# Four graph layers on one core: orders and product forms in the first slices, and layer 3's three weights applied before its first product

## The chip, the cores and the metric

The kernel runs on one core of a Trainium2 chip. The metric is the device time of one execution in microseconds (us); the median of several executions is given with the lowest and the highest. In the profile PE is TensorE's matrix multiplication, PEld its weight loads, DVE the VectorE, ACT the ScalarE, POOL the GpSimd, SP the SyncE, which here only issues transfers. PSUM is the memory into which PE sums, in eight banks of 512 fp32 values for each of 128 partitions.

## The reference, cut to what matters

x is 8 x 2048 x 64 (batch, nodes, features) and adj, called A, is 2048 x 2048 with rows that sum to 1. Everything is fp32. Four layers follow each other, each with a residual and a layernorm over the 64 features:

```python
x = _layernorm(x + _L0_gnn_ref(x, adj, L0_gnn_embedding, L0_gnn_weight, L0_gnn_bias), axis=-1)
x = _layernorm(x + _L1_gnn_ref(x, 0, L1_gnn_net_params, adj), axis=-1)
x = _layernorm(x + _L2_gnn_ref(x, adj, L2_gnn_weight_self, L2_gnn_weight_neighbor, L2_gnn_bias), axis=-1)
x = _layernorm(x + _L3_gnn_ref(x, adj, adj, L3_gnn_weight, L3_gnn_bias), axis=-1)
```

Layer 0 takes x, Ax and 2AAx - x through weights that differ by node. Layer 1 is relu(A x W) twice. Layer 2 is x Wself + (A x) Wneigh + b. Layer 3 is this, with adj for both supports:

```python
x0 = inputs_and_state
x_stack = [x0]
for support in (support0, support1):
    x1 = jnp.einsum('ij,bjk->bik', support, x0)
    x_stack.append(x1)
    x_prev, x_curr = (x0, x1)
    for _ in range(2, K + 1):
        x2 = 2.0 * jnp.einsum('ij,bjk->bik', support, x_curr) - x_prev
        x_stack.append(x2)
        x_prev, x_curr = (x_curr, x2)
x_cat = jnp.concatenate(x_stack, axis=-1)
out = jnp.einsum('bnf,fo->bno', x_cat, weight) + bias
```

With the five 64 x 64 parts W0 to W4 of its weight and both supports alike, layer 3 is x (W0 - W2 - W4) + A x (W1 + W3) + A A x 2 (W2 + W4) + b. The kernel calls these three weights W3X, W3A and W3AA. All weights have their mean over the outputs taken away, so that a layernorm needs no mean, and the identity is added to the weight of x, which gives the residual.

## The kernel before

**Where things lie.** x lies in SBUF by nodes: `xy[:, slot, t, col]`, 128 nodes on the partitions, t one of 16 node tiles, col the 8 x 64 columns of batch and feature; slot 0 and 1 are two such arrays. A pair `p` is two batches (128 columns), a group `g` four node tiles (512 nodes). `part(g, p, slot)` is one 128 x 512 piece.

**Products.** Every A times X is 2048 x 2048 by 2048 x 512. `product` does it in two levels of the seven-product method (Strassen-Winograd): seven quarter products, in the order A11, S1, A12, S2, S4, S3, A22, and in each, `inner` with seven `mul`s. Each `mul` loads one 1 MB block of adj, or of a sum of adj blocks, from DRAM (`comb`, made in the first stage) on SP's queue; seven such buffers are in flight in the later layers. Thus one product is 49 `mul`s. A `mul` has two forms. The form at L277 is 4 matmuls 512 wide with x as the loaded weight; its result is by features and has to go through a weight (`project`) to come back to nodes. The form at L270 (`onto_slot`) is 16 matmuls 128 wide with adj as the loaded weight; its result is by nodes and is added to what already lies in an xy slot. A matmul of the program is two instructions in the trace.

**Order on PE.** Small jobs (transposes, projections) are Python generators in a queue, the pump. After each `mul` the pump takes `rate` steps, so jobs come between the blocks of a product. That order is PE's order in the built program. `prior` adds the jobs of `own` to the pump, one for each quarter of the output.

**First stage (0 to 212 us).** The first A X is made in four slices `ns`, each of 512 output columns, while DVE makes the sums of adj blocks (`prepare`, line L640, names `si` for inner sums and `so` for outer ones) and POOL stores them to `comb`. adj arrives in 1 MB chunks on SP's queue (L158), x on ACT's and SP's (L169, L172). Slice 0 (`plain_slice`) is half plain matmuls (L872), half `two_level` (L832, 28 matmuls 128 wide). Slices 1 to 3 (`fast_slice`) have seven quarter products: A12, A22, A11, S1, S2, S4, S3, of which A22 is by `two_level` and the others are 16 matmuls 256 wide for each of two pairs (L918). `prepare` is a generator; each `next(parts)` lets DVE's queue have the next group of sums. The results hT go back to nodes by transposes (L465), those of the last slice's first pairs after the slice.

**Layer 2 and 3.** `both_terms` (L1177) takes two pairs: it transposes each (L1152, four transposes into one PSUM bank `pt`, copied to SBUF as `xT`), multiplies the upper and the lower 64 rows by two weights of 64 columns side by side (L1190, 16 pairs of half-row matmuls into four banks), and ACT copies one result to slot 0 (L1195), DVE adds the bias to the other and writes slot 1 (L1196). Layer 3 uses `w3o` with W3A for slot 0 and W3X for slot 1. Its first product, of slot 1 in the 512-wide form, gives A x by features; `feature3` (L1213) projects that by W3AA and adds it to slot 0, which then holds x W3A + (A x) W3AA. Its second product, of slot 0 in the 128-wide form, adds A times that to slot 1. `ends` gives the last quarter a special end (layernorm and store piece by piece). PSUM has three banks for the products and five for these jobs (`p_z`).

**Weights.** `load_weights` and `sum_weights` (L594 to L629) build seven 128 x 128 weights `wd` (the 64 x 64 weight twice on the diagonal) and copy four of them into `w2o` and `w3o`; they run on DVE in slice 1.

Of the kernel before, what the change touches and what calls it, by code (L numbers as in the profile page):

```python
# [16 lines left out]
P = 128  # L17
EPS = 1e-5
GW = 512
# [85 lines left out]
def kernel(  # L105
# [58 lines left out]
    AHEAD = (2, 3, 0, 1)  # L164
    chunks[0, AHEAD[0]] = slice_chunk(0, AHEAD[0], (1, 1, 2))

    for t, n, cols in ((0, 1, slice(0, 2 * F)), (0, 1, slice(2 * F, BF)), (1, 1, slice(0, BF)), (2, 2, slice(0, BF))):
        t += AHEAD[0] * TG
        nc.scalar.dma_start(xy[:, 0, t : t + n, cols], x[:, t : t + n, cols])  # L169
# [7 lines left out]

    W1A, W1B, W2N, W2S, W3X, W3A, W3AA = range(7)
    wd = const.tile([P, 7, P], F32, tag="wd", name="wd")

    w3o = const.tile([P, 2, F], F32, tag="w3o", name="w3o")
    w2o = const.tile([P, 2, F], F32, tag="w2o", name="w2o")
    b2 = const.tile([P, F], F32, tag="b2", name="b2")
    b3 = const.tile([P, F], F32, tag="b3", name="b3")
# [400 lines left out]
    if True:  # L585
# [8 lines left out]
        def load_weights():  # L594
            nc.gpsimd.memset(wd, 0.0)
            w3 = sums.tile([P, 5, F], F32, tag="t", name="w3", bufs=5)
            for k in range(2):
                half = slice(k * F, (k + 1) * F)
                for i, src in ((W1A, w_l1[0]), (W1B, w_l1[1]), (W2N, w_neigh), (W2S, w_self)):
                    nc.sync.dma_start(wd[half, i, half], src)  # L600
                nc.scalar.dma_start(w3[half], w_l3.rearrange("(k i) o -> i k o", i=F))
            nc.sync.dma_start(b2, b_l2.to_broadcast([P, F]))
            nc.sync.dma_start(b3, b_l3.to_broadcast([P, F]))
            return w3

        def sum_weights(w3):
            pin = tc.keep_in_program_order

            for k in range(2):
                half = slice(k * F, (k + 1) * F)  # L610
                pin(nc.vector.tensor_tensor(wd[half, W3A, half], w3[half, 1], w3[half, 3], ALU.add))
                pin(nc.vector.tensor_tensor(w3[half, 2], w3[half, 2], w3[half, 4], ALU.add))
                pin(nc.vector.tensor_tensor(wd[half, W3X, half], w3[half, 0], w3[half, 2], ALU.subtract))
                pin(nc.vector.tensor_scalar(wd[half, W3AA, half], w3[half, 2], 2.0, None, ALU.mult))


            for k in range(2):
                half = slice(k * F, (k + 1) * F)
                center(wd[half, W2N:, half], half, pin=pin)
            for w in (W2S, W3X):  # L620
                pin(nc.vector.tensor_tensor(wd[:, w, :], wd[:, w, :], ident, ALU.add))
            for k in range(2):
                half = slice(k * F, (k + 1) * F)
                for n, w in enumerate((W3A, W3X)):
                    pin(nc.vector.tensor_copy(w3o[half, n], wd[half, w, half]))
                for n, w in enumerate((W2N, W2S)):
                    pin(nc.vector.tensor_copy(w2o[half, n], wd[half, w, half]))
            center(b2.unsqueeze(1), pin=pin)
            center(b3.unsqueeze(1), pin=pin)  # L629
# [4 lines left out]
        def prepare(ns, ch, outers):  # L634
# [50 lines left out]
            yield  # L685
            inner(A12, *raw(0, 1))
            if ns == 0:

                sums_of_blocks()
                outers[A11] = inner(A11, *raw(0, 0))  # L690
                outers[A21] = inner(None, *raw(1, 0))
# [7 lines left out]
            put(S1, s1)  # L699
            yield  # L700
            put(S2, s2)
            if ns:
                inner(A11, *raw(0, 0))
            yield
            if ns:
                outers[S3] = s3 = outer(rq(0, 0), rq(1, 0), ALU.subtract)
                yield
            put(S3, s3)
            if ns == 0:
                yield  # L710
            put(S4, s4)
            yield

        with tc.tile_pool(name="p_n", bufs=4, space=PSUM) as p_n, tc.tile_pool(
# [92 lines left out]
            ]  # L807
            t1 = [[by_tiles(xy[:, 1, c:NT:TG, ts(n, 2 * F)]) for n in range(4)] for c in range(2)]
            b4 = [T[3][:, 2 * j : 2 * j + 2, :, ts(p, 2 * F)] for j in range(2) for p in range(2)]
# [86 lines left out]
            def fast_slice(ns, ch, held, rest):  # L896
# [16 lines left out]

                def mul(ps, a, b, start=True, steps=2):

                    for p in range(2):
# [6 lines left out]
                        if p < steps:  # L923
                            pump.step()
                    return ps
# [31 lines left out]
                next(parts)  # L957
                pa = mul(bank(), raw(0, 0), x_of(0, 0))
                p1 = sums.tile([P, GW], F32, tag="p1", name="p1")
                nc.scalar.copy(p1, pa)  # L960
                nc.vector.tensor_tensor(q3, q3, p1, ALU.add)
# [13 lines left out]
                nc.vector.tensor_tensor(u2, pc, u2, ALU.add)  # L975
                nc.vector.tensor_tensor(p1, pc, p1, ALU.add)
                next(parts)
                pe = mul(bank(), summed(S4), x_of(1, 1))
                done(1, pe, u2)
                if ns == TG - 1:  # L980
                    join_bias(1, 0)
                mul(pb_, summed(S3), t_of(3), start=False)

                done(2, pb_, q3)
                done(3, pb_, p1)
                return [hT[p] for p in range(NP)]

            last_pairs = []
            for ns in range(TG):
                ch = [chunks.pop((ns, j)) for j in range(NG)]  # L990
                if ns == 0:
# [15 lines left out]
                    hT = next(first4)  # L1007
                    next(parts)
                    w3 = load_weights()
                    load_chunks(1, *AHEAD)  # L1010
                    pump.add(biases())
                else:
                    hT = fast_slice(ns, ch, held, parts if ns == 1 else ())
                for p in range(NP):
                    keep_t1(ns, p, hT[p])

                held = []
                for p in range(NP):
                    if ns == TG - 2:
                        held.append((ns, p, hT[p]))  # L1020
                    elif ns == TG - 1 and p >= NP // 2:
                        last_pairs.append(hT[p])
                    else:
                        pump.add(back(ns, p, hT[p]))
            join_bias(1, 1)
# [111 lines left out]

    late = p_z = None

    def to_late():  # L1140
# [5 lines left out]
        p_mm2 = ctx.enter_context(tc.tile_pool(name="p_mm2", bufs=1, space=PSUM))  # L1146
        p_z = ctx.enter_context(tc.tile_pool(name="p_z", bufs=5, space=PSUM))

    def pair_transposed(g, p, slot):
        pt = p_z.tile([P, GW], F32, tag="z", name="pt2")  # L1150
        for k in range(TG):
            nc.tensor.transpose(pt[:, ts(k, P)], xy[:, slot, g * TG + k, ts(p, 2 * F)], ident)  # L1152
        xT = late.tile([P, GW], F32, tag="xT", name="xT", bufs=2)
        nc.scalar.copy(xT, pt)
# [48 lines left out]
    def nothing(g, p, c):  # L1203

        yield from ()


    product(1, then(feature1b, 0, mean=True, after=both_terms(0, w2o, b2)), rate=2)
    product(0, then(nothing, 1), onto_slot=1)


    def feature3(g, p, hT):
        nc.vector.tensor_tensor(part(g, p, 0), project([(hT, W3AA)]), part(g, p, 0), ALU.add)  # L1213
        yield

    product(1, feature3, own=both_terms(1, w3o, b3), rate=1.5)
    product(0, then(nothing, 1, single=[(1, 0)], store=True), rate=2, onto_slot=1, ends=True)
    pump.drain()
# [47 lines left out]
```

## Time and profile before

| what | value |
| --- | --- |
| median of 3 executions | 1666.83 us (1666.49 to 1666.88) |
| profiled execution | 1666.76 us |
| its span | 1665.0 us |
| granted clock of TensorE, mean | 0.999 |
| bytes moved by DMA | 391.56 MB |
| first stage, first A X | 0 to 212 us |
| layer 0's second product with its weights | 212 to 736 us |
| layer 1, two products | 736 to 1092 us |
| layer 2's product | 1092 to 1276 us |
| layer 3's first product | 1276 to 1482 us |
| layer 3's second product and end | 1482 to 1665 us |

A line of the timeline has start, duration, engine, source line, operation, output<-inputs by the program's names, the shape (rows and columns of the loaded weight, then output), and how many instructions in a row it stands for; square brackets give the idle time before it and what ended it. A window line has, for each engine, its busy time and instructions, then the granted clock, the DMA share and GB/s. A DMA line has the queue, the number of transfers, their size and the median time from issue to landing in us.

### The profile page before, as it was taken

How to read it: one execution, taken by the hardware profiler on the slowest of the kernel's cores; microseconds unless marked ns; L12 is line 12 of the kernel's file. 1: busy time of each engine (PE TensorE's matmuls, PEld its weight loads, DVE VectorE, ACT ScalarE, POOL GpSimd, SP SyncE). 2: the span in 40 equal slices, each digit the busy share in tenths (PEclk: the TensorE clock that was granted, in tenths of full speed). 3: DMA queues.
4: the chain of work that ended last, by engine and by line, in shares of the span. 5: the costliest groups of instructions: out<-in, count | busy, mean ns of one | idle time of the engine just before them, and what ended most of it. 6: DMA issues, size and time to landing. Idle time of an engine off the chain costs nothing.

```text
span 1665.0 us, 21271 instructions
## 1 busy us (share of the span) xinstructions
PE 1656.7 (100%) x8414; PEld 1060.6 (64%) x8414; DVE 965.9 (58%) x1737; ACT 276.0 (17%) x810; POOL 246.1 (15%) x332
## 2 busy tenths in 40 slices
PE   9999999999999999999999999999999999999998
PEld 5988844444444444444454455599998455579998
DVE  5986895656456456655434365873668344453657
ACT  0200110242142144430010011220001011100001
POOL 1221200254155056550000000000000000000000
PEclk9999999999999999999999999999999999999999
DMA  8998899504503600019877867657888866678884
GB/s 318 340 383 310 316 322 326 200 26 162 205 26 129 250 26 26 26 65 364 290 266 278 304 254 257 229 218 272 291 297 299 306 209 233 230 264 294 316 311 167
DMA packets 81074, 391.56 MB, mean 235 GB/s; under 512 B 8944, under 2 KB 25584, under 8 KB 41040
## 3 DMA queue, kind: packets, MB, share of 16 engines
q1 hardware_dynamic: 68288, 346.78, 58.2%
q0 software_dynamic: 11248, 42.08, 6.7%
q10 hardware_dynamic: 1440, 1.35, 0.3%
q8 instruction: 67, 1.10, 0.3%
q14 instruction: 31, 0.25, 0.0%
HBM read 339.85 MB, written 50.33 MB: 234 GB/s over the span
## 4 chain that ended last, share of the span: by engine, by line
PE 95%; DVE 3%; DMA 1%; issue 0%; SPq 0%; DVEq 0%
PE y L1109 20%; PE mmb L277 17%; PE mma L277 12%; PE mmc L277 12%; PE mmb L270 9%; PE ps_n L918 7%; PE mma L270 6%; PE mmc L270 6%; PE z L1161 3%; PE z L1190 2%; PE ps_i L832 1%; DVE si L640 1%; DMA xy<-in_x 1%; PE pt L1152 1%; DMA bias<-in_b_l 0%; DVE so L640 0%
## 5 line engine op out<-in xcount | busy, mean ns | idle before, releaser
L277 PE MATMUL mmb<-a,t 128*128 128x512 f32 x648 | 292.0, 593 | 0.0
L1119 DVE SCALAR_TENSOR_TENSOR xy<-y,e_sb,xy 128x128 f32<-128x128 f32 x512 | 179.6, 351 | 141.2 <-PE y L1109 125.3
L277 PEld LDWEIGHTS mmb<-a,t 128*128 128x128 f32 x648 | 121.5, 190 | 145.3 <-issue 143.5
L1128 POOL TENSOR_TENSOR s<-s 128x512 f32<-128x512 f32 (+2 forms) x192 | 157.4, 820 | 333.0 <-ACT s L1123 322.8
L1123 ACT ACTIVATE s<-y,e_sb 128x128 f32<-128x128 f32 x512 | 139.3, 383 | 231.5 <-PE y L1109 231.5
L228 DVE TENSOR_TENSOR u<-mmb,p 128x512 f32<-128x512 f32 x84 | 57.9, 689 | 176.5 <-PE mmb L277 121.1
L270 PE MATMUL mmb<-t,a 128*128 128x128 f32 x1344 | 156.9, 275 | 0.0
L270 PEld LDWEIGHTS mmb<-t,a 128*128 128x128 f32 x1344 | 153.5, 192 | 0.0
L1109 PE MATMUL y<-wn,xT 64*128 64x512 f32 x512 | 131.5, 590 | 0.0
L1109 PE MATMUL y<-wn,C 64*128 64x512 f32 x512 | 131.2, 589 | 0.0
L1109 PE MATMUL y<-wn,tT 64*128 64x512 f32 x512 | 131.2, 589 | 0.0
L277 PE MATMUL mma<-a,T 128*128 128x512 f32 x256 | 115.5, 594 | 0.0
L277 PE MATMUL mmc<-a,t 128*128 128x512 f32 x216 | 97.3, 592 | 0.0
L295 ACT COPY p<-mma 128x512 f32<-128x512 f32 x42 | 24.7, 588 | 405.8 <-PE mma L277 248.4
L1109 PEld LDWEIGHTS y<-wn,xT 64*128 64x128 f32 x512 | 49.3, 187 | 61.2 <-issue 60.7
L1109 PEld LDWEIGHTS y<-wn,tT 64*128 64x128 f32 x512 | 49.6, 187 | 60.2 <-issue 60.2
L1109 PEld LDWEIGHTS y<-wn,C 64*128 64x128 f32 x512 | 49.5, 187 | 60.3 <-issue 60.3
L277 PE MATMUL mma<-a,xy 128*128 128x512 f32 x192 | 86.6, 594 | 0.3 <-PE pt_n L465 0.3
L277 PEld LDWEIGHTS mma<-a,T 128*128 128x128 f32 x256 | 47.6, 190 | 56.8 <-issue 56.5
L228 DVE TENSOR_TENSOR C<-mmc,C 128x512 f32<-128x512 f32 x48 | 33.2, 692 | 85.9 <-PE mmc L277 75.1
L277 PEld LDWEIGHTS mmc<-a,t 128*128 128x128 f32 x216 | 40.0, 190 | 45.4 <-issue 45.2
L277 PEld LDWEIGHTS mma<-a,xy 128*128 128x128 f32 x192 | 36.0, 190 | 44.4 <-issue 43.8
(160 smaller groups left out, 2127.5 us busy)
## 6 DMA issues: line engine op xcount, KB each, us to landing
a<-comb SPq DMA_DIRECT2D x240, 1024.0 KB, 4.8
a<-in_blocks SPq DMA_DIRECT2D x54, 1024.0 KB, 4.8
comb<-si POOLq DMA_DIRECT2D x28, 1024.0 KB, 6.2
a<-in_slices SPq DMA_DIRECT2D x15, 1024.0 KB, 9.0
comb<-so POOLq DMA_DIRECT2D x15, 512.0 KB, 9.6
t1T<-hT SPq DMA_DIRECT2D x16, 256.0 KB, 4.6
xT<-in_xT SPq DMA_DIRECT2D x16, 256.0 KB, 3.0
tT<-t1T SPq DMA_DIRECT2D x16, 256.0 KB, 3.1
```

Source lines behind the costliest of these rows:

```text
L228: nc.vector.tensor_tensor(out, a, b, op)
L270: nc.tensor.matmul(to, a[:, k, m, :], xb[:, m, :], start=(start and opens and m == 0), stop=(m == TG - 1), skip_group_check=True,)
L277: nc.tensor.matmul(ps, xb[:, m, :], a[:, :, m, :], start=(start and m == 0), stop=(m == TG - 1), skip_group_check=True,)
L295: nc.scalar.copy(p1, pa)
L640: tc.keep_in_program_order(nc.vector.tensor_tensor(out, a, b, op))
L918: nc.tensor.matmul(ps[:, ts(p, GW // 2)], b(k, p), a(k // TG, k % TG), start=(start and p == k == 0), stop=(k == NT // 2 - 1), skip_group_ ...
L1109: mm = nc.tensor.matmul(y[:, b, :], terms[n][half, ts(k, P)], wn[half, n, h * DH : (h + 1) * DH, :], start=(n == 0), stop=(n == 2),)
L1119: nc.vector.scalar_tensor_tensor(acc, y[:, :, ts(d, F)], e, acc, ALU.mult, ALU.add)
L1123: nc.scalar.activation(s[:, d], y[:, :, ts(d, F)], AF.Copy, scale=e)
L1128: nc.gpsimd.tensor_tensor(s[:, :n], s[:, :n], s[:, n : 2 * n], ALU.add)
L1161: nc.tensor.matmul(z[:, k, :], aT[:, ts(k, P)], wd[:, w, :], start=(n == 0), stop=(n == len(terms) - 1),)
L1190: nc.tensor.matmul(z[n][:, k], xT[half, ts(k, P)], w[half], start=True, stop=True)
```

## The change

In the first stage: the first adj chunk comes in pieces of 1 and 3 tiles (before: 1, 1, 2), and x's tiles 1 to 3 of the first chunk in one transfer of 768 KB (before: 256 and 512 KB). In slice 0, `put`, which makes and stores the inner sums, comes in the order S1, S3, S2, S4; S2 and S4 are made while slice 1 begins. In slice 1, A11 goes through `two_level` as A22 does, so its inner sums are made earlier. In the last slice S3 comes ahead of S4, and the transposes of pairs 0 and 1 are stepped inside S4's matmuls. `wd` keeps two weights; `w2o` and `w3o` are loaded and summed where they are used, `w3o` with three weights.

In layer 3: `three_terms`, stepped from the pump after layer 2's layernorm of each pair, transposes a pair, multiplies it by the three weights W3AA, W3A, W3X side by side (192 columns) in upper and lower row halves, copies x W3AA to slot 0 and x W3A to slot 1 (ACT), adds the bias to x W3X (DVE) and stores that to DRAM (`x3`, POOL's queue, 16 x 256 KB). The first product is then A (x W3AA), in the 128-wide form, added to slot 1. Meanwhile x3 is loaded to slot 0 (POOL's queue). The second product is A times slot 1, added to slot 0. PSUM is shared out anew: while `three_terms` runs, one bank for transposes and two tiles of two banks for sums; afterwards two banks. `xT` and `rest` share three buffers.

```diff
-    chunks[0, AHEAD[0]] = slice_chunk(0, AHEAD[0], (1, 1, 2))
-    for t, n, cols in ((0, 1, slice(0, 2 * F)), (0, 1, slice(2 * F, BF)), (1, 1, slice(0, BF)), (2, 2, slice(0, BF))):
+    chunks[0, AHEAD[0]] = slice_chunk(0, AHEAD[0], (1, 3))
+    for t, n, cols in ((0, 1, slice(0, 2 * F)), (0, 1, slice(2 * F, BF)), (1, 3, slice(0, BF))):
...
             inner(A12, *raw(0, 1))
+            if ns == 1:
+                outers[A11] = inner(A11, *raw(0, 0))
...
             put(S1, s1)
             yield
+            if ns == 0:
+                put(S3, s3)
+                yield
             put(S2, s2)
-            if ns:
+            if ns > 1:
                 inner(A11, *raw(0, 0))
...
-                pa = mul(bank(), raw(0, 0), x_of(0, 0))
-                p1 = sums.tile([P, GW], F32, tag="p1", name="p1")
-                nc.scalar.copy(p1, pa)
+                p1 = new_out("p1")
+                if ns == 1:
+                    two_level(
+                        lambda i, j: lambda m: ch[j][:, m, i], outers[A11], b1[0], t1[0], by_blocks(p1)
+                    )
+                else:
+                    pa = mul(bank(), raw(0, 0), x_of(0, 0))
+                    nc.scalar.copy(p1, pa)
...
                 if ns == TG - 1:
+                    nc.vector.tensor_tensor(q3, pb_, q3, ALU.add)
+                    next(parts)
+                    ps3 = mul(bank(), summed(S3), t_of(3))
+                    done(2, ps3, q3)
+                    for p in range(2):
+                        keep_t1(ns, p, hT[p])
+                        pump.add(back(ns, p, hT[p]))
+                    done(3, ps3, u2)
                     join_bias(1, 0)
-                mul(pb_, summed(S3), t_of(3), start=False)
+                    pe = mul(bank(), summed(S4), x_of(1, 1), n=2)
+                    done(1, pe, u2)
...
+    def to_wide():
+        nonlocal p_z, p_zz
+        banks_z.close()
+        p_z = banks_z.enter_context(tc.tile_pool(name="p_z1", bufs=1, space=PSUM))
+        p_zz = banks_z.enter_context(tc.tile_pool(name="p_zz", bufs=2, space=PSUM))
...
+    def three_terms(g, p):
+        tiles = tiles_of(g)
+        xT = pair_transposed(g, p, 1)
+        yield
+        for q in range(2):
+            rest = late.tile([P, GW], F32, tag="xT", name="rest", bufs=3)
+            rest4 = rest.rearrange("p (a b n f) -> p a b n f", a=2, b=2, n=2)
+            zs = [p_zz.tile([P, 2, GW], F32, tag="zz", name="zz") for _ in range(2)]
+            zs = [z[:, :, : 6 * F].rearrange("p a (b n f) -> p a b n f", b=2, n=3) for z in zs]
+            for k in range(TG):
+                for n in range(2):
+                    half = slice(n * F, (n + 1) * F)
+                    nc.tensor.matmul(
+                        zs[n][:, k // 2, k % 2], xT[half, ts(k, P)], w3o[half], start=True, stop=True
+                    )
+            if q == 0:
+                xT = pair_transposed(g, p + 1, 1)
+            for n, z in enumerate(zs):
+                cols = ts(2 * (p + q) + n, F)
+                for slot in range(2):
+                    to = xy[:, slot, tiles, cols].rearrange("p (a b) f -> p a b f", b=2)
+                    nc.scalar.copy(to, z[:, :, :, slot])
+                nc.vector.tensor_tensor(
+                    rest4[:, :, :, n], z[:, :, :, 2],
+                    b3.unsqueeze(1).unsqueeze(1).to_broadcast([P, 2, 2, F]), ALU.add,
+                )
+            nc.gpsimd.dma_start(x3[g, p + q], rest)
+            yield
...
-    product(0, then(nothing, 1), onto_slot=1)
-    def feature3(g, p, hT):
-        nc.vector.tensor_tensor(part(g, p, 0), project([(hT, W3AA)]), part(g, p, 0), ALU.add)
+    product(0, then(nothing, 1, after=three_terms), to_wide, rate=1.5, onto_slot=1)
+    def rest_of(g, p):
+        for q in range(2):
+            nc.gpsimd.dma_start(part(g, p + q, 0), x3[g, p + q].rearrange("p (t c) -> p t c", t=TG))
         yield
-    product(1, feature3, own=both_terms(1, w3o, b3), rate=1.5)
-    product(0, then(nothing, 1, single=[(1, 0)], store=True), rate=2, onto_slot=1, ends=True)
+    product(0, nothing, own=rest_of, onto_slot=1)
+    product(1, then(nothing, 0, single=[(1, 0)], store=True), to_ends, rate=2, onto_slot=0, ends=True)
```

## The prediction

> **What bounds the kernel now.** I read the busy times first, then the chain, then stage windows, and last the timelines of TensorE around each edited place.
>
> ```profile
> PE 1656.7 (100%) x8414; PEld 1060.6 (64%) x8414; DVE 965.9 (58%) x1737; ACT 276.0 (17%) x810; POOL 246.1 (15%) x332
> ...
> PE 95%; DVE 3%; DMA 1%; issue 0%; SPq 0%; DVEq 0%
> ```
>
> TensorE (PE) is busy 1656.7 of 1665.0 us and holds 95% of the chain. What is not PE is small: 1.06 us at the start, two short waits shown below, and the 6.7 us of layernorm and store after the last product. So a change is worth what it adds to or takes from PE's row of instructions, plus the waits it makes. DVE's 3% of the chain lies at 24 to 69 us: the sums of adj blocks in the first slices. The stage in which layer 3 now starts:
>
> ```profile
> 1276.30:1482.30 206.00, 206.00 (x835) 108.84 (x834) 94.77 (x158) 26.24 (x61) 0.00 (x0) 1.00 0.70 251
> ```
>
> The columns are PE (busy, after the window's sum), weight loads, DVE, ACT, POOL, granted clock, DMA share, GB/s. PE is full at clock 1.00, DVE is 46% busy (94.77/206), ACT 13%, POOL idle, the DMA engines 70%. Work moved to DVE, ACT or POOL here is covered by PE unless PE waits for a buffer of it. Three places on PE:
>
> ```profile
> 1276.28 3.60 PE L277 MATMUL mma<-a,xy 128*128 128x512 f32 x8
> 1324.35 3.60 PE L277 MATMUL mma<-a,xy 128*128 128x512 f32 x8
> ...
> 1360.56 1.05 PE L1161 MATMUL z<-wd,C 128*128 128x128 f32 x8
> 1361.45 1.04 PE L1152 MATMUL pt<-ident,xy 128*128 128x128 f32 x8
> 1362.33 3.60 PE L277 MATMUL mmb<-a,t 128*128 128x512 f32 x8
> 1365.86 2.06 PE L1190 MATMUL z<-w3o,xT 64*128 64x128 f32 x32
> 1367.84 3.70 PE L277 MATMUL mma<-a,T 128*128 128x512 f32 x8
> 1371.38 1.04 PE L1152 MATMUL pt<-ident,xy 128*128 128x128 f32 x8
> ...
> 1504.61 3.74 PE L270 MATMUL mmc<-xy,a 128*128 128x128 f32 x32
> 1533.20 3.74 PE L270 MATMUL mma<-xy,a 128*128 128x128 f32 x32
> ```
>
> Starts matter here, not durations, since matmuls overlap. From 1276.28 to 1324.35 are 14 loaded blocks in the 512-wide form: 48.07/14 = 3.434 us each. From 1504.61 to 1533.20 are 8 in the 128-wide form: 28.59/8 = 3.574 us. A projection z<-wd,C costs 1361.45 - 1360.56 = 0.89, four transposes 1362.33 - 1361.45 = 0.88 us. From 1362.33 to 1371.38 are two blocks and one set of layer 3's row-half products (16 pairs, each a product on the upper and one on the lower 64 rows): 9.05 - 2 x 3.434 = 2.18 us.
>
> **Layer 3: what goes.** Sixteen projections by W3AA: 16 x 0.89 = -14.2 us. Eight sets of row-half products: 8 x 2.18 = -17.4 us. The 64 transposes remain (16 x 0.88 both ways).
>
> **Layer 3: what comes.** The first product there, 49 blocks, turns from the 512-wide into the 128-wide form: 49 x (3.574 - 3.434) = +6.9 us. `three_terms` brings 16 sets of 4 pairs with 192 columns (three weights at once). The trace has no 192-wide pair. Below it: 128-wide matmuls start every 0.1117 us (at 68 us, 56 in 6.25 us), and 16 pairs at that pitch are 1.79 us, which leaves 2.18 - 1.79 = 0.39 us for going into the 64-row form and back. Above it, in the first stage:
>
> ```profile
> 97.28 13.98 PE L918 MATMUL ps_n<-so,xy 128*128 128x256 f32 x64
> 111.09 3.62 PE L918 MATMUL ps_n<-a,xy 128*128 128x256 f32 x16
> ```
>
> 64 matmuls of 256 columns in 13.81 us are 0.2158 each. A matmul of the program is two instructions here, and in the 64-row form upper and lower run side by side, so 8 matmuls are 8 steps of such a pitch. Midway for 192 columns: 0.1637. One set: 8 x 0.1637 + 0.39 = 1.70 us, 16 sets +27.2 us. Bounds: no 0.39 at each set (21.0 us), or the 256-column pitch throughout (33.9 us). I take the middle, because the edge was seen in each of the eight old sets and 192 lies halfway.
>
> The Trainium skill, TensorE: Matmul & The Clock Gate, section on LDWEIGHTS, gives a load's time by its columns alone, about 107 ns for 128 of them, whatever its rows. Two loads for each half-row pair would then be 213 ns against 164 of streaming, and my estimate from that page is another 16 x 8 x 0.049 = 6.3 us. The row speaks against it: the old pairs start every 112 ns with two loads each. Left out of the sum.
>
> So layer 3 by counts is -14.2 - 17.4 + 6.9 + 27.2 = +2.5 us: the count of matmuls falls, but the edge is paid 16 times in place of 8, and the 128-wide form costs 0.14 us a block.
>
> **Layer 3: emptying PSUM.** `three_terms` has two tiles of two banks for the sums (upper, lower), and one bank for transposes, where there were five banks in one pool. The old block empties like this:
>
> ```profile
> 1367.94 0.65 ACT L1195 COPY xy<-z 128x256 f32<-128x256 f32 x2 [0.24 <-PE z L1190]
> ...
> 1367.77 1.41 DVE L1196 TENSOR_TENSOR xy<-z,b 128x256 f32<-128x256 f32 x4
> ```
>
> Copies start 0.27 us apart, each 0.38; four adds in 1.41. A new set needs four copies and two adds: after its last product 0.30 + 3 x 0.27 + 0.38 = 1.49 us for ACT, and some 0.4 for DVE's add behind it, so about 1.95. Where a block of the product (3.57) stands between two sets, that is covered. In the built order one pair of sets in the quarter tile 01 and one in 11 has only four transposes and two matmuls between, about 1.2 us: 0.75 us of wait each. DVE may be in a 0.69 us add just then (half the time: 2 x 0.17), and twice a transpose finds the single bank not yet copied (0.3 each). Sum 1.5 + 0.3 + 0.6 = +2.4 us, bounds 0 and 6 (both sets waiting for a full DVE queue of four adds). If this cover goes elsewhere too, each of the 14 others costs up to 1.9.
>
> **Put at nothing.** DVE gets 32 adds and loses 32 adds and 16 of feature3; ACT gets 64 copies and loses 32: covered at 46% and 13% busy. POOL gets 16 stores of `rest` and 16 loads of 256 KB, 8.4 MB, beside 70 to 77% DMA share. The loads of x3 land in slot 0 ahead of additions in the next product's quarters; POOL has nothing else queued then. SP's queue of 1 MB blocks is seven deep, 7 x 3.5 = 25 us ahead, so a slower block isn't felt. Without that cover 8.4 MB at 251 GB/s would be 33 us of DMA time. Fewer DVE operations on weights (6 to 4 us, in slice 1) and the joined PSUM pools touch no PE work.
>
> **First slices.** Slice 1's A11 changes from 16 matmuls of 256 columns x 2 (32 x 0.2158 = 6.91) to `two_level` (56 x 0.1117 = 6.25): -0.7. Two waits go:
>
> ```profile
> 69.37 1.13 PE L832 MATMUL ps_i<-si,t 128*128 128x128 f32 x8 [0.31 <-DVE si L640]
> ...
> 211.71 3.67 PE L277 MATMUL mma<-a,xy 128*128 128x512 f32 x8 [0.27 <-PE pt_n L465]
> ```
>
> The first was 0.48 late against a pitch of 0.89 (start to start 1.37). S4's sums now go behind the slice, so A22's come 2.5 us sooner: -0.5. What is late next is A11: its sums are made on DVE at 75.4 in place of these first `so`:
>
> ```profile
> 75.41 2.35 DVE L640 TENSOR_TENSOR so<-a 128x1024 f32<-128x1024 f32 x2
> ```
>
> Two 0.69 us sums after it put the second at about 76.8 where PE wants it at 75.4: +1.1 to 1.5. The second wait (211.71 - 209.99 = 1.72 against 0.87) goes because pairs 0 and 1 are transposed inside the last S4: -0.8. At the start, x tiles 1 to 3 come in one 768 KB transfer:
>
> ```profile
> xy<-in_x ACTq DMA_DIRECT2D x1, 512.0 KB, 10.2
> xy<-in_x ACTq DMA_DIRECT2D x1, 256.0 KB, 8.0
> ```
>
> Tile 1 landed at 9.7 us and PE used it at 9.9, so a common transfer that lands with or after the old 512 KB one (12.3) could hold PE by 0 to 2.5 us. Such a hold gives DVE the same time, so it and A11's wait are not added: the larger counts, and I take +1.3 for both (0 to 2.5). Slices together: -0.7 - 0.5 - 0.8 + 1.3 = -0.7 us.
>
> **Sum.** +2.5 + 2.4 - 0.7 = +4.2 us. The profiled execution took 1666.76 us, span 1665.0 and 1.76 around it; the median of the runs is 1666.83, 0.07 above. 1666.8 + 4.2 = 1671.0 us. A run of this kernel can tell about 0.2% (3.3 us) from no change.
>
> **Rivals.**
> No change: PSUM is emptied in time, since DVE is more than half idle, and A11's sums perhaps aren't late. The sum is then 2.5 - 0.7 = 1.8, or 0.5 without the late A11: 1667.3 to 1668.6 us. For it: 46% DVE. Against: DVE was 98% busy up to 120 us, where A11's sums lie, and two sets stand too close to each other. Chance 0.27.
> Slower by the stores: transposed pairs and `rest` share three buffers, so the second following add waits until a store has landed. From a set's end at +2.0 us to the add that wants the buffer at +7.05 are 5 us. A 256 KB store on POOL took:
>
> ```profile
> comb<-so POOLq DMA_DIRECT2D x15, 256.0 KB, 9.8
> ```
>
> That is in the first stage at DMA share 0.91; near 4 us in the quiet one. At 9.8, two close sets cost 4.9 each and three spaced ones 1.3 each: +13, so 1684 us. It decides from about 5 us. Late stages stand at 0.70 to 0.77, between the two. Chance 0.15. The Trainium skill, DMA: Bandwidth & Descriptors, on POOL's transfers, gives about 2 us and bytes by 436 GB/s: an estimate of 2.6 us by that page, with which this case never happens.
> Faster: the 0.39 us edge isn't paid by new sets, which stand beside transposes in part, and nothing waits. 27.2 becomes 21.0, the stall 0: 4.2 - 6.2 - 2.4 = -4.4, so 1662.4 us. It decides below an edge of about 0.05 us a set. Against: the edge stood in each old block, beside a full product block on both sides. Chance 0.08.
>
> **How the numbers follow.** The forecast, slower by pitch and edges, has 0.50, and rivals 0.27, 0.15, 0.08. Slower by over 0.2%: 0.50 + 0.15 = 0.65; within: 0.27; faster: 0.08. The range runs from 1665.5, below no change, to 1680, into the stores' case; the forecast's own is 1669 to 1675.
>
> **What would show it.** Sets of `zz` 1.70 us on PE between neighbours; blocks of layer 3's first product 3.57 us apart; waits of `zz` on DVE's `rest` add below 1 us each in quarters 01 and 11 and nowhere else; one wait of about 1 us at A11 in slice 1; no gap at 210 us; DMA share up by 0.02 to 0.05 in the late stages. Wrong it is if sets cost under 1.4 us or over 2.1, if PE waits at every set, or if the first matmuls wait for x beyond 2.5 us.

## The result and the profile after

The changed kernel took 1676.82 us (median of 4 executions, 1675.69 to 1679.03) against 1666.74 us before: ratio 1.0061, 95% interval 1.0048 to 1.0074. That is 10 us slower, on the side that was forecast and inside the full range of 1665.5 to 1680 us, but above the forecast's own 1669 to 1675 us and more than twice the 4.2 us of the sum. The profiled execution took 1676.06 us, its span is 1674.3 in place of 1665.0 us: +9.3 us. So these 9.3 us can be followed line by line; the rest up to the median is differences between executions, which are taken up below.

The page's busy times and chain:

```profile
PE 1658.6 (99%) x9486; PEld 1154.0 (69%) x9486; DVE 966.9 (58%) x1729; ACT 286.0 (17%) x848; POOL 265.9 (16%) x364
...
PE 23%; DVE 0%; ACT 0%; issue 0%; DVEq 0%
```

PE's busy time rose by only 1.9 us, so 7.4 of the 9.3 us are time in which PE stood still: 15.7 us now, 8.3 before. The chain adds up to 23%, so it was followed back over the last quarter of the span and breaks off there. It can't be used for the rest. The list of PE's waits (what waited, for what, us in total, times, longest) covers the whole span:

```profile
PE ps_n L872 <- DMA xy<-in_x: 3.3, 2, 1.8
PE zz L1253 <- DVE rest L1263: 1.8, 2, 1.7
PE ps_i L832 <- DVE si L637: 1.7, 1, 1.7
PE rise L724 <- DVE zero L721: 1.1, 1, 1.1
PE mma L278 <- PE ps_n L918: 0.9, 1, 0.9
PE ps_i L832 <- ACT part L836: 0.4, 1, 0.4
```

Four waits are new: for x at the very start, for A11's sums (`si`) and a bank copy in slice 1, and in layer 3 for the addition `rest`. The start of the same piece of work in both timelines of PE shows where the time came in:

| start of, us | before | after | later by |
| --- | --- | --- | --- |
| bias products, slice 1 | 62.51 | 65.16 | 2.65 |
| A11 of slice 1 | 74.80 | 76.90 | 2.10 |
| layer 1's first product | 211.71 | 215.94 | 4.23 |
| layer 2's product, one and the same place | 1086.70 | 1090.93 | 4.23 |
| last matmul | 1658.15 | 1667.68 | 9.53 |

Between 216 and 1091 us nothing changed. The first stage cost 4.2 us, for which -0.7 was forecast, and layer 3 cost 5.3 us, for which +4.9 was forecast. PE's timeline at A11 and, below, DVE's at the same time, with the issue of one store on POOL:

```profile
76.90 1.06 PE L832 MATMUL ps_i<-a,xy 128*128 128x128 f32 x8
78.31 0.49 PE L832 MATMUL ps_i<-a,xy 128*128 128x128 f32 x2 [0.35 <-ACT part L836]
80.49 1.16 PE L832 MATMUL ps_i<-si,xy 128*128 128x128 f32 x8 [1.69 <-DVE si L637]
...
85.73 3.62 PE L918 MATMUL ps_n<-so,T 128*128 128x256 f32 x16
```

```profile
75.91 0.69 DVE L637 TENSOR_TENSOR si<-a,si 128x512 f32<-128x512 f32 x1
79.02 0.69 DVE L637 TENSOR_TENSOR si<-a 128x512 f32<-128x512 f32 x1 [2.43 <-DMA comb<-si]
79.74 0.69 DVE L637 TENSOR_TENSOR si<-si,a 128x512 f32<-128x512 f32 x1
...
71.82 0.75 POOL L646 DMA_DIRECT2D comb<-si  x1 [1.78 <-DVE si L637]
```

A11 took 85.73 - 76.90 = 8.83 us, 1.9 more than the 6.91 of the old form, where 0.7 less was forecast. Without waits it would be 6.25 us, so its waits cost 2.6. The second `si` ends at 80.43 and PE goes on at 80.49. DVE itself stood still for 2.43 us ahead of A11's sums: they need one of four buffers, and that one was S2's, whose store was issued on POOL at 71.82 and landed at 78.99 us by its semaphore. So the sums were late because of a store, not because DVE had too much to do.

At the end of the first stage another wait changed. Before, then after, DVE's last additions there and PE's first weight load of layer 1's product:

```profile
210.87 0.75 DVE L934 TENSOR_TENSOR hT<-ps_n,p 128x256 f32<-128x256 f32 x2
211.68 0.30 PEld L277 LDWEIGHTS mma<-a,xy 128*128 128x128 f32 x2 [0.48 <-PE pt_n L465]
...
215.09 0.75 DVE L934 TENSOR_TENSOR hT<-ps_n,u 128x256 f32<-128x256 f32 x2 [0.17 <-PE ps_n L918]
215.91 0.30 PEld L278 LDWEIGHTS mma<-a,xy 128*128 128x128 f32 x2 [1.26 <-PE ps_n L918]
```

The profile names PE's own last work as what ended the wait, but that had ended 0.24 us earlier before and 0.86 us earlier after. In all thirteen profiles the load starts 0.07 us after the second of DVE's additions, which take the last product out of PSUM. So the product waits for DVE to empty those banks, in both orders. In the new order no transposes fill this time: from the start of PE's last matmul to that of the next are 1.27 us, 1.05 above the pitch of 0.22, where before 0.85 were lost. These pieces add up to the first stage's 4.2 us: 2.65 at the start, -0.55 for A22's wait, 1.9 at A11, 0.2 here.

In layer 3 one set of `three_terms` between blocks of the product, and the one long wait:

```profile
1276.38 0.61 PE L271 MATMUL mma<-T,a 128*128 128x128 f32 x4
1278.67 1.90 PE L1253 MATMUL zz<-w3o,xT 64*128 64x192 f32 x16 [1.68 <-DVE rest L1263]
...
1283.72 3.74 PE L271 MATMUL mmb<-t,a 128*128 128x128 f32 x32
1287.39 1.57 PE L1253 MATMUL zz<-w3o,xT 64*128 64x192 f32 x16
1288.89 3.84 PE L271 MATMUL mmc<-t,a 128*128 128x128 f32 x32
1292.56 3.74 PE L271 MATMUL mmb<-t,a 128*128 128x128 f32 x32
```

From 1283.72 to 1292.56 are two blocks and one set: 8.84 - 2 x 3.574 = 1.69 us for the set, where 1.70 was worked out. The wait stands where it was expected: after the set at 1274.38 come only four transposes and two matmuls. DVE's timeline shows what it waited for:

```profile
1275.67 0.68 DVE L229 TENSOR_TENSOR u<-mmb,p 128x512 f32<-128x512 f32 x1
1276.27 0.68 DVE L229 TENSOR_TENSOR t<-xy,t 128x512 f32<-128x512 f32 x1
1276.87 0.68 DVE L229 TENSOR_TENSOR C<-C,u 128x512 f32<-128x512 f32 x1
1277.59 0.69 DVE L229 TENSOR_TENSOR C<-xy,C 128x512 f32<-128x512 f32 x1
1278.19 0.75 DVE L1263 TENSOR_TENSOR rest<-zz,b 128x256 f32<-128x256 f32 x2
```

The set's last product had ended at 1275.95; the two `rest` additions stood behind four others in DVE's queue.

### The profile page after: what moved, and what is told of

Same layout as the page of the kernel before. It is cut to its first block, busy times and chain, and to the rows that moved or that the text cites. A ratio compares the mean times of both kernels' runs of the same rounds, so it can differ in the third digit from the quotient of the medians.

```text
span 1674.3 us, 23571 instructions
## 1 busy us (share of the span) xinstructions
PE 1658.6 (99%) x9486; PEld 1154.0 (69%) x9486; DVE 966.9 (58%) x1729; ACT 286.0 (17%) x848; POOL 265.9 (16%) x364
## 5 line engine op out<-in xcount | busy, mean ns | idle before, releaser
L271 PE MATMUL mmb<-t,a 128*128 128x128 f32 x2016 | 236.0, 275 | 0.0
L271 PEld LDWEIGHTS mmb<-t,a 128*128 128x128 f32 x2016 | 230.4, 192 | 0.2 <-issue 0.2
L278 PE MATMUL mmb<-a,t 128*128 128x512 f32 x480 | 215.8, 592 | 0.0
L278 PEld LDWEIGHTS mmb<-a,t 128*128 128x128 f32 x480 | 90.3, 190 | 109.5 <-issue 108.5
L271 PE MATMUL mma<-T,a 128*128 128x128 f32 x768 | 90.0, 275 | 0.0
L271 PEld LDWEIGHTS mma<-T,a 128*128 128x128 f32 x768 | 87.8, 192 | 0.3 <-issue 0.2
L278 PE MATMUL mma<-a,T 128*128 128x512 f32 x192 | 86.5, 593 | 0.0
L271 PE MATMUL mmc<-t,a 128*128 128x128 f32 x672 | 78.7, 275 | 0.0
L271 PEld LDWEIGHTS mmc<-t,a 128*128 128x128 f32 x672 | 76.7, 192 | 0.5 <-issue 0.5
L278 PE MATMUL mmc<-a,t 128*128 128x512 f32 x160 | 72.1, 592 | 0.0
```

Of the source, the lines that this page charges most:

```text
L271: nc.tensor.matmul(to, a[:, k, m, :], xb[:, m, :], start=(start and opens and m == 0), stop=(m == TG - 1), skip_group_check=True,)
L278: nc.tensor.matmul(ps, xb[:, m, :], a[:, :, m, :], start=(start and m == 0), stop=(m == TG - 1), skip_group_check=True,)
```

## The experiments

Eleven more kernels were run. Each time is a median beside runs of before on the same chip (1666.4 to 1666.7 us). "First product" is the start of layer 1's first product in the profile, "the rest" from there to the last matmul.

| kernel | median us (lowest to highest) | ratio to before, 95% | first product | the rest |
| --- | --- | --- | --- | --- |
| before | 1666.4 to 1666.7 | | 211.71 | 1446.44 |
| after | 1676.82 (1675.69 to 1679.03) | 1.0061 [1.0048, 1.0074] | 215.94 | 1451.74 |
| layer3_only | 1671.21 (1670.94 to 1672.73) | 1.0027 [1.0016, 1.0038] | 211.13 | 1451.75 |
| slices_only | 1672.62 (1670.76 to 1672.96) | 1.0033 [1.0020, 1.0045] | 217.48 | 1446.44 |
| old_start | 1675.23 (1674.55 to 1676.36) | 1.0053 [1.0039, 1.0066] | 214.53 | 1451.75 |
| a11_first | 1673.17 (1672.86 to 1674.98) | 1.0040 [1.0027, 1.0053] | 214.82 | 1451.75 |
| a12_last | 1670.73 (1669.81 to 1672.24) | 1.0026 [1.0016, 1.0036] | 209.47 | 1453.32 |
| adj_merged | 1673.10 (1671.44 to 1673.22) | 1.0034 [1.0021, 1.0048] | 211.47 | 1453.34 |
| x_merged | 1672.65 (1670.88 to 1673.82) | 1.0037 [1.0023, 1.0051] | 210.57 | 1453.33 |
| rest_on_act | 1670.38 (1670.21 to 1671.06) | 1.0024 [1.0015, 1.0032] | 210.87 | 1451.08 |
| all_mended | 1669.91 (1669.19 to 1671.40) | 1.0019 [1.0011, 1.0028] | 209.71 | 1451.08 |
| slices_mended | 1665.45 (1665.22 to 1666.29) | 0.9995 [0.9986, 1.0004] | 210.07 | 1446.44 |
| slices_mended_old_end | 1665.87 (1665.09 to 1666.16) | 0.9996 [0.9987, 1.0005] | 210.62 | 1446.44 |

**The two halves apart.** layer3_only is before with the change's weights and layer 3; slices_only is before with the change's first stage.

> The first stage of before with layer 3 of the change. Theory (the two parts are separate; in the profile of after the part from layer 2's product to the end took 5.3 us more on PE and the tail 0.2 less): 1666.7 + 5.1 = 1671.8 us, one PE wait of 1.7 us at a zz set behind DVE's rest. Rival (the late part's size depends on what the first stage left, such as the transfers of the sums): more than 1 us off that.

> The first stage of the change with layer 3 of before. Theory: layer 1's product starts 4.2 us later than before (2.65 at the first x tiles, 2.4 at A11's sums in slice 1, less the shorter A11 and A22's wait), and nothing of it is made up: 1666.7 + 4.2 = 1670.9 us. If the spread of the changed kernel's times (1675.7 to 1679.0) comes from the transfers at the start and at A11, this one has the spread and layer3_only has not.

layer3_only came to +4.65 us. Its rest is 1451.75 us, that of after to a hundredth, so layer 3's cost of 5.3 us does not depend on the first stage. Its first stage is 0.6 us shorter than before, because the old wait for A22's sums is gone in this profile. That is no gain of the change: an x transfer landed 0.66 us earlier, DVE, which waits for it, went on at 23.10 in place of 23.76 us, and A22's sums started 0.66 us earlier. The weight operations that DVE no longer has come later, from some 94 us on. In rest_on_act, with the same first stage, PE came 1.0 us earlier and the wait is back with 0.5 us. slices_only came to +6.06 us, 1.7 more than expected, and its profile says why. This is PE in slices_only (start, duration, instructions, wait) and then windows of it (PE, weight loads, DVE, ACT, POOL, granted clock, DMA share, GB/s):

```profile
7.43 2.84 PE L875 MATMUL ps_n<-a,xy 128*128 128x512 f32 x6 [0.24 <-DMA xy<-in_x]
12.31 12.24 PE L875 MATMUL ps_n<-a,xy 128*128 128x512 f32 x24 [2.03 <-DMA xy<-in_x]
```

```profile
12.30:13.20 0.90, 0.89 (x2) 0.46 (x3) 0.00 (x0) 0.66 (x1) 0.00 (x0) 1.00 1.01 383
13.20:14.20 1.00, 1.00 (x3) 0.44 (x2) 0.00 (x0) 0.62 (x1) 0.00 (x0) 0.52 1.04 395
14.20:15.20 1.00, 1.00 (x3) 0.48 (x2) 0.12 (x1) 0.00 (x0) 0.00 (x0) 0.50 1.01 406
15.20:16.20 1.00, 1.00 (x2) 0.41 (x2) 0.97 (x2) 0.00 (x0) 0.00 (x0) 0.50 1.11 418
16.20:17.20 1.00, 1.00 (x3) 0.32 (x2) 1.00 (x3) 0.00 (x0) 0.00 (x0) 0.77 0.89 328
```

After the wait of 2.03 us the granted clock fell to 0.50 for some 3.4 us, and four matmuls started 0.85 us apart in place of 0.43: 1.7 us lost once more. In the profile of after, two waits of 1.5 and 1.8 us at the same place left the clock at 1.00. So the same wait costs 1.7 us extra in some executions and nothing extra in others; the last section shows what decides. The lowest of slices_only's five times, 1670.76 us, has a mean clock of 0.999 where the other four have 0.998, and lies next to the 1670.9 us expected. The spread doesn't separate the two halves: both kernels' times spread over some 2 us.

**The start.** old_start is the changed kernel with the first pieces as before:

```diff
-    chunks[0, AHEAD[0]] = slice_chunk(0, AHEAD[0], (1, 3))
+    chunks[0, AHEAD[0]] = slice_chunk(0, AHEAD[0], (1, 1, 2))
...
-    for t, n, cols in ((0, 1, slice(0, 2 * F)), (0, 1, slice(2 * F, BF)), (1, 3, slice(0, BF))):
+    for t, n, cols in ((0, 1, slice(0, 2 * F)), (0, 1, slice(2 * F, BF)), (1, 1, slice(0, BF)), (2, 2, slice(0, BF))):
```

> The changed kernel with the first pieces of adj and x as before (1, 1, 2 tiles; 256 and 512 KB). Theory (A11's sums on DVE wait for a buffer whose store lands at 79 us whatever PE did before, so PE's loss at the start is hidden by that wait): the wait for x goes, A11's wait grows by as much to some 4.5 us, time within 0.5 us of the changed kernel's. Rival (the two waits add up): 2.6 us faster than the changed kernel.

The theory fell, and the median, 1.6 us below after's, lies between it and the rival. The waits for x went and slice 1's bias products started at 61.98 us, 3.2 earlier than in after, but A11's wait did not grow:

```profile
77.45 1.89 PE L832 MATMUL ps_i<-si,xy 128*128 128x128 f32 x8 [1.82 <-DVE si L637]
79.13 1.49 PE L832 MATMUL ps_i<-a,xy 128*128 128x128 f32 x6
```

The same wait is 1.72 us in slices_only, where the bias products start at 66.67. So whether the start lost nothing, 2.7 or 4.2 us, A11's wait stayed, and the two losses add up. DVE's sums had moved ahead together with PE: A22's first sum starts at 64.53 in place of 66.38, A11's at 75.98 in place of 79.02 us. Of these 3.0 us, 1.4 are a wait of DVE in after that old_start has not, for a copy of a product of slice 0:

```profile
43.35 0.56 DVE L847 TENSOR_TENSOR u<-u,part 128x384 f32<-128x384 f32 x1 [1.38 <-ACT u L836]
```

So a part of PE's loss is handed to DVE. Another 0.5 us are an adj chunk that landed earlier (DVE's first sum at 15.07 in place of 15.54), and 1.2 the store of S2's sums, which took 5.98 in place of 7.18 us; no run shows why these two moved. Only 1.4 of the 3.2 us were left at the first product: in this execution A11's wait was the one that halved the clock. Eight matmuls there took 1.89 us where after has 1.16, and the windows from 77.4 to 81.4 us have clocks of 0.64, 0.50, 0.50 and 0.66.

**A11's sums.** a11_first only changes DVE's order in slice 1:

```diff
-            inner(A12, *raw(0, 1))
             if ns == 1:
                 outers[A11] = inner(A11, *raw(0, 0))
+            inner(A12, *raw(0, 1))
```

> The changed kernel with slice 1's A11 sums ahead of A12's on DVE, so that A11 takes A12's buffer and place (74 in place of 79 us) and A12 waits for S2's store instead. Theory (the store of S2's sums holds A11): PE's 1.7 us wait at A11 goes, S1's sums end at 83.9 as before and PE wants them at 83.6: 1.9 to 2.3 us faster than the changed kernel. Rival (DVE's queue as a whole is late there): the wait moves to S1 in full, no gain.

Both waits at A11 went and none came at S1; from the bias products to layer 1's first product are 148.2 us in place of 150.8, 2.6 less. The median is 3.6 us below after's. That is more than the wait, but the medians hold falls of the clock: a11_first's profiled execution, its slowest (1674.98), has one at the start, where after's (1676.06) has none, and the other four lie at 1672.86 to 1673.26 us, some 2.9 below after's profiled one. a12_last takes both remedies, with A12's sums behind S4's:

```diff
             if ns == 1:
                 outers[A11] = inner(A11, *raw(0, 0))
-            inner(A12, *raw(0, 1))
+            else:
+                inner(A12, *raw(0, 1))
...
             outers[S4] = s4 = outer(rq(0, 1), sq(s2), ALU.subtract)
+            if ns == 1:
+                inner(A12, *raw(0, 1))
```

> The changed kernel with the old first pieces, and in slice 1 DVE's sums in the order A11, S1, S2, S4, A12. Theory (PE's losses before 212 us are the start, the store that A11's sums wait for, and halved clock after each such wait): no wait for x, A11's wait under 0.3 us, S1's sums there in time, no drop of the clock before 212 us; first product at about 211.6 us as against 214.5 in old_start, time 1670.0 us (old_start less 2.1 of wait, 1.8 of halved clock, and 0.5 of the bank copy if that goes too). Rival (DVE's whole queue is late): PE waits at S1 or A22 instead and the time stays at 1672.5 or more.

After the first 1.1 us no wait is left before 208 us and the first product starts at 209.47, 6.5 us earlier than in after and 2.2 earlier than before (0.9 of these 2.2 because slice 0's first product began at 5.06 in place of 5.92 us). The rest of it is longer than in other kernels, 1453.32 against 1451.75 us, because here it was the wait at the `zz` set that halved the clock:

```profile
1273.00:1274.00 1.00, 1.00 (x12) 0.78 (x8) 0.00 (x0) 0.19 (x1) 0.30 (x1) 0.94 0.15 57
1274.00:1275.00 1.00, 1.00 (x5) 0.92 (x5) 0.42 (x1) 1.00 (x4) 0.00 (x0) 0.50 0.53 205
1275.00:1276.00 1.00, 1.00 (x7) 1.00 (x7) 0.42 (x1) 0.01 (x1) 0.24 (x1) 0.50 0.00 0
1276.00:1277.00 1.00, 1.00 (x6) 1.00 (x6) 0.00 (x0) 0.00 (x0) 0.30 (x1) 0.50 0.14 57
```

**Which piece at the start.** adj_merged is a12_last with adj in pieces of 1 and 3 tiles, x_merged is a12_last with x's 768 KB transfer.

> As a12_last, but the first adj chunk in pieces of 1 and 3 tiles as in the change; x in its old pieces. If the larger adj piece takes the bandwidth of the 192 KB piece of x beside it: PE waits 1.5 us for x at its first tile, none at tile 1, and the clock may drop (0 to 1.7 us): 1.0 to 3.2 us slower than a12_last. If only x's own 768 KB transfer hurts: same as a12_last.

> As a12_last, with x's tiles 1 to 3 in one 768 KB transfer as in the change and adj in its old pieces. If x's transfer holds PE by itself: no wait at tile 0, one of 1.8 to 2.6 us at tile 1 (12.3 against 9.7 us), and the clock may halve after it: 1.8 to 4 us slower than a12_last. If the two merges hurt only together: as a12_last.

adj's larger piece hurts by itself: the 192 KB piece of x issued beside it lands at 7.5 in place of 5.9 us, PE waits 0.7 us there and 0.2 at tile 1, and the median is 2.4 us up. Slice 1's bias products start 2.0 us later, 0.7 of it because this execution's first product began later (5.78 in place of 5.06 us) before any wait. For x's larger transfer alone it is not shown. PE waits 0.6 us at tile 1, less than expected, since the transfer landed at 9.6 and not at 12.4 us; the bias products start 1.1 us later (0.4 of it from a later first product), the median is 1.9 us up. But slices_mended_old_end has a wait of 0.7 us there with x's old pieces, whose 256 KB piece took 6.7 to 8.8 us in nine kernels, and x_merged's 768 KB took 7.9. With both merged the 768 KB took 10.4 to 10.7 us in three kernels, and in after the waits were 1.5 and 1.8 us.

**The wait in layer 3.** rest_on_act is layer3_only with this edit:

```diff
-                nc.vector.tensor_tensor(
-                    rest4[:, :, :, n], z[:, :, :, 2],
-                    b3.unsqueeze(1).unsqueeze(1).to_broadcast([P, 2, 2, F]), ALU.add,
-                )
+                nc.scalar.copy(rest4[:, :, :, n], z[:, :, :, 2])
+            flat = rest.rearrange("p (k f) -> p k f", f=F)
+            nc.vector.tensor_tensor(flat, flat, b3.unsqueeze(1).to_broadcast([P, 2 * TG, F]), ALU.add)
```

> layer3_only, in which ACT copies the third term to rest too (six copies a set) and DVE adds the bias later in SBUF, so that PSUM is emptied by ACT alone. Theory (the 1.7 us wait is the rest add standing behind four adds in DVE's queue): the bank is free after 1.8 us of ACT in place of 2.7, wait down to about 0.9 us, time 0.7 to 1.0 us under layer3_only. Rival (emptying itself is the bound, or ACT is late): wait the same or longer, and more sets wait.

The median fell by 0.83 us and the rest by 0.67. In PE's waits the 1.8 us behind DVE are replaced by this:

```profile
PE zz L1235 <- ACT rest L1245: 0.4, 2, 0.2
```

That is 0.2 us ahead of each of the two close sets. Both sets then take 2.32 us from start to start in place of 1.50, since their upper and lower products start up to 0.27 us apart and not 0.007, which is why 1.4 us less at the head gave only 0.67. So DVE's queue held the bank in the long wait; with ACT alone its copies are what the next wait is put down to. Why the products inside a close set no longer start side by side was not tested.

**Everything mended.** all_mended is a12_last together with rest_on_act.

> a12_last together with rest_on_act: the whole change with its long waits taken away. Theory (a12_last's times lie in two groups, near 1669.9 and 1672.1, because the 1.7 us wait at a zz set halves the clock in some executions): with no wait of PE over 0.5 us all times lie within 1 us, at 1669.2 us; layer 3 still takes 4.6 us more than before by its counts and short waits. Rival (the groups come from elsewhere, the transfers for one): still two groups.

Ten of eleven times lie between 1669.19 and 1670.36 us, one at 1671.40, and the median is 0.7 above the expected; the two groups of a12_last are gone. That the clock made these groups is borne out by its mean over each execution: 0.998 in a12_last's four slower ones, 0.999 to 1.000 in the four faster. all_mended's one at 1671.40 has 0.999 and is not explained. Layer 3 still takes 1451.08 - 1446.44 = 4.6 us more than before, as expected. So the remaining loss is layer 3's, against a first stage that is now 2.0 us shorter than before's in this profile; 1.0 of it lies between the bias products and the first product, and 0.45 is again an earlier begin of slice 0.

**The first stage without layer 3.** slices_mended has before's layer 3 and weights, the slices of the change, old first pieces and DVE's order of a12_last. slices_mended_old_end also has the last slice as before.

> Layer 3 and weights of before, the slices of the change with the old first pieces and the DVE order of a12_last. Theory: 1666.6 less A22's wait 0.5 and A11's 0.7, plus 0.2 at the handover to layer 1's first product and 0 to 0.8 of A11's remaining waits: 1665.6 to 1666.4 us. Rival (the two halves are not separate): over 1667 us.

> slices_mended with the last slice as before (S4, then S3, and the transposes of pairs 0 and 1 behind it). By the prediction's term the new order saves 0.8 us there, so this would be 1666.3 us. By the profile of after the new order only puts another wait in its place (1.05 in place of 0.85 us above the pitch): this would be 0.2 us faster than slices_mended, 1665.3 us.

slices_mended took 1665.45 us where before took 1666.42 beside it. It and its sister are the only versions with a median below that of before as well as after, clearly below after, but the intervals to before (0.9986 to 1.0004 and 0.9987 to 1.0005) take in no change. The last slice can't be told by the medians: in the second kernel's profile one x tile came 0.7 us late although its pieces are the old ones. By the traces, from the bias products to the first product are 148.21 us with the new end and 147.99 with the old one, so the old end is 0.2 us shorter.

## Why the prediction was right, and where it was not

The direction was right, and layer 3, which made 5.3 of the profile's 9.3 us, was right by its terms. That the whole came out inside the range was partly luck: the range reached 1680 us for the rival of the stores, which did not happen, and the first stage and the clock filled it. One of the prediction's own signs of being wrong came true: the first matmuls waited 3.3 us for x in two waits, beyond 2.5.

**Layer 3: right by its terms.** Projections -14.2: -14.3 by their starts in before. A new set 1.70: measured 1.69, of which 8 x 0.1625 are the pairs (from start to start inside a set; 0.1637 was interpolated) and 0.39 the edge, as in the old sets. So the bound without the edge lost, and so did the rule that would have added 6.3 us for weight loads: the two loads of a half-row pair did not set its pitch. The waits ahead of the close sets came to 2.4 us, as forecast (1.75 and 0.23 ahead of the two sets, 0.23 twice ahead of a transpose), but unevenly: one set met four additions, which had stood as the bound, the other almost none. What the sum left out lies inside these two sets: they took 1.83 and 2.05 us from start to start in place of 1.50, 0.9 us together. With it the terms add up to 5.5 of the measured 5.3 us; forecast were 4.9. One reading was off without effect on the total: the row of 0.88 us holds eight transposes, not four, since a transpose is one instruction in the trace. Four take 0.44 us, so the close sets stood 0.95 us apart and not 1.2, while the transposes that remain still cancel out.

**The first stage: wrong, -0.7 forecast, +4.2 measured in the profile.** Step by step:

"Such a hold gives DVE the same time, so it and A11's wait are not added: the larger counts" is the step that failed. The start cost 2.65 us, just over its bound of 2.5, A11's waits 2.6 us, and they added where 1.3 was taken for both. The wait of 1.4 us that PE's slice 0 gave DVE is a part of the reason; for the rest no run shows one. The lateness of A11's sums was worked out from DVE's operations alone (1.1 to 1.5 us). The runs showed a buffer instead: four of them, 1 MB stores of 7.2 us each, and a fifth user. The form itself was right: in a12_last, without waits, A11 takes 6.25 us.

"The second wait ... goes because pairs 0 and 1 are transposed inside the last S4: -0.8" failed, because that wait was not for the transposes. The first product waits for DVE's last additions in both orders, and lost 1.05 us there, 0.2 more than before.

A22's wait did go (0.55 gained, 0.5 forecast).

**What had no term at all: the clock.** The sum gave each wait its own length. In six of the thirteen profiles a wait of 1.7 to 2.0 us was followed by 3.4 us at clock 0.50, worth another 1.6 to 1.8 us. After's four times, 1675.69, 1676.06, 1677.58 and 1679.03, would fit none, none, one and two such falls. Only the profiled one (1676.06) can be seen, and it has none; the slowest one's mean clock of 0.997, against 0.999 to 1.000 in the others, agrees, but for the third it does not tell. So the step from the profile's +9.3 us to the median's is likely the clock's, not shown.

**The rivals.** Stores held no set: `rest` landed in 2.8 us in the median (2.3 to 7.5), near the 2.6 us estimated, and no PE or DVE wait for them appears. (The rival's own terms give 13.7 us, not 13.) The DMA share rose from 0.78 to 0.81 between 1482 us and the last matmul, within the 0.02 to 0.05 expected, but from 0.70 to 0.82 between 1276 and 1482 us, without a wait of PE for it. "No change" fell with the waits. The faster case fell with the edge, which was paid at 0.39 us a set.

## What to carry to other kernels

Before a step is moved forward on an engine, count the buffers between it and the stores that free them, not only the engine's time. Two late inputs of one engine can add up when the engine that makes the second also waits for the first one's work, so don't count only the larger. When a profile names as the end of a wait work that ended long before, look for what ended just before it. A wait of 2 us on TensorE may cost nearly twice its length, so a kernel with no long wait is worth more than its sum.

## What the runs showed of the hardware

The granted clock fell to one half after idle stretches of TensorE of only 1.67 (a12_last), 1.68 (adj_merged, x_merged), 1.82 (old_start), 1.95 (a11_first) and 2.03 us (slices_only), and it did so in some executions and not in others: after's profile has waits of 1.83, 1.69 and 1.68 us with the clock at 1.00 behind each. So length doesn't decide. What does can be read from the traces. All rises and falls of the clock lie on a raster of 3.413 us: in slices_only it rises at 6.42, falls at 13.24 and rises at 16.66 us, two steps and one; in a12_last it rises at 4.11 and falls at 1273.87, 372 steps later. Fourteen waits of 1.4 us or more lie in the profiles:

| waits | where on the raster | clock after |
| --- | --- | --- |
| slices_only 10.27 to 12.31 | whole between 9.83 and 13.24 | falls at 13.24 |
| a11_first 10.29 to 12.24 | whole between 9.73 and 13.15 | falls at 13.15 |
| old_start 75.62 to 77.45 | whole between 74.26 and 77.68 | falls at 77.68 |
| a12_last 1270.52 to 1272.19 | whole between 1270.46 and 1273.87 | falls at 1273.87 |
| adj_merged 1272.52 to 1274.19 | whole between 1271.98 and 1275.39 | falls at 1275.39 |
| x_merged 1271.62 to 1273.30 | whole between 1271.38 and 1274.79 | falls at 1274.79 |
| eight others: four in after, one each in layer3_only, slices_only, old_start, a11_first | a mark inside the wait | stays at 1.00 |

In each execution the raster begins elsewhere (the first rise lies between 3.89 and 6.99 us), so the same wait hits a mark in one and none in the next. This is read off fourteen waits; no run moved a wait on purpose to test it. The Trainium skill, TensorE: Matmul & The Clock Gate, section on the HAM clock gate, lets the clock fall after at least one idle window of about 3.4 us, and says that the window runs freely, so that what is seen differs from run to run. The second agrees with these runs, as does the length of the half-speed stretch (3.413 us); the first doesn't, and the measurement decides: 1.67 us was enough here.

A transfer's time depended on its neighbour's size: the same 192 KB piece of x took 4.5 to 5.1 us beside a 256 KB piece of adj (nine kernels) and 6.2 to 6.6 us beside a 768 KB piece (four kernels).
